# Attention by halves of the heads with the scores four rounds ahead, and a feed-forward second pass in written order with one PSUM bank per chunk

## The chip, the cores and the metric

The kernel runs on one core of a Trainium2 chip. The metric is the device time of one execution in microseconds. The core's engines are PE (TensorE, matrix products and transposes), DVE (VectorE), ACT (ScalarE), POOL (GpSimd) and SP (SyncE, which issues DMAs). Each works off its own queue in order; semaphores tie the queues together. [...]

## The reference, cut to what matters

Two layers are applied to `x` of shape (16, 256, 256), 16 batches of 256 rows. All products below are in fp32 unless another type is named.

```python
# layer 0: masked attention of 16 heads of 16 columns, keys = values = ctx
scores = einsum('bqhd,bkhd->bhqk', layernorm(x) by heads, ctx by heads)
scores = where(mask == 0, -1e20, scores)
out = softmax(scores / 16) @ ctx by heads
x = x + out @ W_out.T + b_out

# layer 0: quantised feed-forward, 256 -> 1024 -> 256
# quant_act: s = max(t) / 255 over the WHOLE tensor; round(t / s) clipped to 0..255
h = relu(quant_act(layernorm(x)) @ int8(w1).T + b1)
x = x + quant_act(h) @ int8(w2).T + b2

# layer 1: attention by lags: the correlation of q and k over all circular lags,
# the six best lags over the batch mean, a softmax over them, v delayed by each lag
x = x + delayed_sum(layernorm(x) @ Wq, ctx @ Wk, ctx @ Wv) @ Wo + bo
# layer 1: mixture of experts, 8 experts of which each row takes 2, and a shared one
x = x + shared(x) + routed(x)
```

The largest value of `h` over all rows is needed before any of `h` can be rounded. So the feed-forward part computes its first product twice: once to find the maximum, once to use it.

## The kernel before, in words

The rows lie in `x` as 32 tiles of 128; a batch is two tiles (`QT` = 2) and a feed-forward block is four tiles of 128 rows (`NB` = 8 blocks). The span has four stages: attention to about 426 us, feed-forward to about 580 us, the lag attention to about 641 us, and the mixture of experts to the end, which the diff does not touch.

**Attention.** A batch `b` is prepared by `prep`: `cxp` (L433) is the context spread out for the heads, `qp` (L442) the normalised rows, `kT` and `qT` are their transposes on PE, copied out of PSUM by ACT (`turn`, L371 and L376; from batch 3 on `turn_close`, L387), and `mbT` (L481, L482) is the transposed mask. The softmax needs the largest score of each row and head. `largest(b, r)` computes a quarter of the scores: eight matmuls `sp` (L500) into two tiles of two banks of the pool `ps_w` (three such tiles), and eight maxima on DVE (L511) into `mx`. Before, `qt, gp = divmod(r, 2)`, so quarters 0 and 1 are the two halves of the heads for the first tile of rows. `shift(b)` takes the finished maxima: DVE writes them negated into `mxc` (L531), PE transposes it (`mxtp`, L540), and DVE adds the result to `qT` (L549, one instruction of 128 x 1024). After that `weights(b, g)` can run: the shifted scores `st` (L568), the mask added by matmuls (L578), and two exps on ACT (L588, `pT`). `values(b, g)` multiplies them with the context (`o`, L601; copied to `oT`, L610). `finish(b)` transposes (`otp`, L619), divides by the sums (`ri` L626, `on` L627, DVE), transposes again (`ontp`, L637), projects (`pp`, L651) and adds to `x` (L655, DVE). `summary` takes layer-norm statistics and a row maximum (`rmax`, L663). 

The 64 rounds `n = 4b + r` are written by hand, and PE keeps the written order: one list of jobs for each of the four slots of a batch. `largest` runs five rounds ahead, at the front of a slot. In slot 3 of batch `b` stand, in order: `largest(b+2, 0)`, `shift(b+1)`, the values of the round before, the weights of this round with a piece of `finish` between its exps. The order on DVE, ACT, POOL and SP is a scheduler's, which starts from the order of emission and heeds priorities (`high_priority`) and `issue_after`; `behind()` puts side work behind the last maximum emitted. Side work is spread over the slots: `rest`, the preparation of other weights on PE (`turn_weight`, eight and four pieces; `product` and the bias row `bvo`, L299 to L306, a chain on DVE), `ints` (rounding of the int8 weights on DVE, L189 to L213), and `ahead` (statistics of later batches). All small transposes share one bank (tag "m").

**Startup.** `prep(0)`, then scores of rounds 0 to 3 of batch 0 with `prep(1)` between them, then `shift(0)`, then the loop.

**Feed-forward.** The first pass computes `ph` (two matmuls `first`, L916, for each of eight chunks and each block) in tiles of two banks, and DVE takes maxima (`hmax`, L1013, one for two chunks). Between them `keys1` turns the context of a batch into keys for layer 1 (`ctp` L931, `cT` L934, `pk` L944, `gT` L952); ten in the pass, two after it. `values1` (`pv`, L961 and L963) does the same for values. A chain on DVE and POOL (L1030 to L1051) then turns the maximum into scales. In the second pass PE has no written order: `hidden` computes two chunks into one two-bank tile (`ps_h`, two tiles), ACT applies the relu (L1060), DVE rounds (`hq`, L1068). `second` multiplies by `w2` (`py`, L1076), ACT writes `yT` (L1083), PE transposes it (`ytp`, L1092), DVE adds it to `x` (L1097) and takes statistics.

**Lag attention.** Normalised rows `xn` are transposed (`x2tp`, L1179) and multiplied; three `values1` stand before it, seven cover the choice of the lags and a DMA of the matrices `cm` (L1303), which the products `po` (L1307) wait for.

Of the kernel before, what the change touches and what calls it, by code (L numbers as in the profile page):

```python
# [18 lines left out]
P = 128  # L19
# [9 lines left out]
def tile_kernel(ctx: ExitStack, tc: tile.TileContext, io: dict, out: bass.AP):  # L29
# [121 lines left out]
    with tc.tile_pool(name="pa", bufs=2) as pa, tc.tile_pool(  # L151
# [69 lines left out]
        def turn_weight(wT, who):  # L221
            while who not in integers:
                yield
            q = integers[who]
            oc_n, ic_n = q.shape[1], q.shape[2] // P
            for oc in range(oc_n):
                for i0 in range(0, ic_n, 4):
                    n = min(4, ic_n - i0)
                    tp = mtile([P, n, P], f"wt_{who}_{oc}_{i0}", BF16)
                    for i in range(n):  # L230
                        nc.tensor.transpose(
                            tp[:, i, :], q[:, oc, (i0 + i) * P : (i0 + i + 1) * P], ident16
                        )
                    nc.scalar.copy(wT[:, i0 : i0 + n, oc * P : (oc + 1) * P], tp)
                    if oc + 1 == oc_n and i0 + n == ic_n:
                        integers[who + "_turned"] = True
                    yield
# [39 lines left out]
        def pair_weights():  # L277
# [22 lines left out]
            nc.vector.memset(bvo3, 0.0)  # L300
            for i in range(3):
                part = pa.tile([P, D], BF16, tag="bvo_part", bufs=1, name=f"bvo_part{i}")
                nc.vector.tensor_copy(part, left)
                nc.vector.tensor_copy(bvo3[32 * i : 32 * i + 1, :], part[32 * i : 32 * i + 1, :])
                if i < 2:
                    nc.vector.tensor_tensor(left, left, part, ALU.subtract)  # L306
            yield
# [18 lines left out]
        def stats_ahead():  # L326

            yield
            yield
            for b0, b1 in [(3, 4)] + [(b, b + 2) for b in range(4, B, 2)]:  # L330
                for b in range(b0, b1):
                    for t in range(b * QT, (b + 1) * QT):
                        ln_stats(mv0, t)
                    yield
                ln_rstd(rstd0, mv0, b0 * QT, (b1 - b0) * QT, "0", scale)
                yield
                for _ in range(0 if b0 == 3 else 5):
                    yield
# [27 lines left out]
        def turn(dst, src, g0, name):  # L366

            tp = mtile([P, 2, QT, P], f"{name}_tp")
# [50 lines left out]
        def prep(b):  # L419
# [32 lines left out]
            with behind():  # L452
                nc.vector.tensor_scalar(mb, mi, 0.0, MASKED, ALU.is_equal, ALU.mult)
# [13 lines left out]
            else:  # L467
                turn(kT, cxp, 0, f"kT{b}")
                yield
                turn(kT, cxp, 2, f"kT{b}")  # L470
                yield
            if b == 0:
                turn(qT, qp, 0, f"qT{b}")
                yield
                turn(qT, qp, 2, f"qT{b}")
                yield
# [9 lines left out]
            if 0 < b < 3:  # L486
# [5 lines left out]
        def largest(b, r):  # L492

            pr = seqs[b]
            qt, gp = divmod(r, 2)
# [11 lines left out]
            for j in range(4):  # L507
                for g in range(2):
# [12 lines left out]
                    if j == 1:  # L521
                        order["half"] = done

        def shift(b):
# [3 lines left out]
            if b < 2:  # L528
                nc.gpsimd.memset(mxc, 0.0)
            with tc.high_priority():  # L530
                nc.vector.tensor_scalar(  # L531
                    mxc[:, :, :, HD : HD + G],
                    pr["mx"].rearrange("p t (g j) -> p t j g", g=G),
# [4 lines left out]
            tp = mtile([P, QT, P], f"mxtp{b}")  # L538
# [4 lines left out]
            with ExitStack() as where:  # L543
                where.enter_context(tc.high_priority())
                if b > 0:
                    where.enter_context(tc.issue_after(order["half"]))
                for gs in (slice(0, 1), slice(1, G)) if b == 0 else (slice(0, G),):
                    to = pr["qT"][:, gs, :]
                    done = nc.vector.scalar_tensor_tensor(  # L549
                        to,  # L550
                        to,
                        keep,
                        tp.rearrange("p t q -> p (t q)").unsqueeze(1).to_broadcast(to.shape),
                        ALU.mult,
                        ALU.add,
                    ).ins
            if b == 0:
                order["last"] = done
# [33 lines left out]
        def values(b, g, pTs):  # L592

            pr = seqs[b]
            if g == 0:
                pr["oT"] = pa.tile([P, G, S], F32, tag="oT", name=f"oT{b}")
            if g % 2 == 0:
                pr["o"] = ps_o.tile([P, 2, S], F32, tag="o", name=f"o{b}_{g}")
            for k in range(QT):
# [9 lines left out]
            if g % 2 == 1:  # L609
# [67 lines left out]
        first_prep = prep(0)  # L677
        piece(first_prep)
        load_x(1, 2)
        for _ in range(3):  # L680
            piece(first_prep)
        largest(0, 0)
        piece(first_prep)
        with behind():
            stats0(1, 2)
        first_prep = prep(1)
        piece(first_prep)
        largest(0, 1)
        piece(first_prep)
        piece(first_prep)  # L690
# [4 lines left out]
        largest(0, 3)  # L695
# [106 lines left out]
        for _ in shift(0):  # L802
            pass
        with behind():
            stats0(2, 3)
        load_x(5, 9)
        pend = None
        for b in range(B + 1):
            nxt = prep(b + 2) if b + 2 < B else rest
# [4 lines left out]
            jobs = [  # L814
                ((nxt,), (rest,), (fin,)),
                ((nxt,), (nxt,), (fin,)),
                ((fin,), (rest,), (fin,)),
                ((shf,), (), (fin,)),
            ]
            if b == 0:  # L820
                jobs = [
                    ((), (), (first_prep,)),
                    ((nxt,), (nxt,), (nxt,)),
                    ((nxt,), (nxt,), (rest,)),
                    ((rest,), (shf,), (rest,)),
                ]
            for r in range(4):

                n = 4 * b + r
                front, later = {0: ([], [4]), 1: ([5], [6])}.get(  # L830
                    n, ([n + 5] if n + 5 < 4 * B else [], [])
                )
                for m in front:
                    largest(*divmod(m, 4))
                for job in jobs[r][0]:
                    piece(job)
                if pend is not None:
                    values(*pend)
                for job in jobs[r][1]:
                    piece(job)  # L840
                pend = (b, r, []) if b < B else None
                wts = weights(*pend) if b < B else None
                piece(wts)
                for job in jobs[r][2]:
                    piece(job)
                piece(wts)
                if n == 0:
                    piece(first_prep)
                for m in later:
                    largest(*divmod(m, 4))  # L850
                with behind():
# [3 lines left out]
                    if b > 0 and r != 2:  # L855
                        piece(ints)
                if r == 0 and b % 4 == 0 and b + 9 < B:
# [3 lines left out]
        for _ in rest:  # L861
            pass
# [19 lines left out]
    with tc.tile_pool(name="pb", bufs=2) as pb, tc.tile_pool(  # L882
        name="ps_h", bufs=2, space=PSUM
    ) as ps_h, tc.tile_pool(name="ps_b", bufs=2, space=PSUM) as ps_b, tc.tile_pool(
        name="ps_y", bufs=2, space=PSUM
    ) as ps_y:
# [27 lines left out]
        def first(blk, ph, fc):  # L914
            for c in range(DC):
                nc.tensor.matmul(  # L916
# [5 lines left out]
                )  # L922
# [59 lines left out]
        def integers_of(blk):  # L982
            qi = pb.tile([P, TB, D], BF16, tag="qi", name=f"qi{blk}")
            for i in range(TB):
                t = blk * TB + i
                u = pb.tile([P, D], F32, tag="u", bufs=4, name=f"u{t}")
# [16 lines left out]
        with tc.manual_schedule(engines={mybir.EngineType.PE}):  # L1003
            for _ in integers_of(0):
                pass
            key = None
            for blk in range(NB):
                ahead = integers_of(blk + 1) if blk + 1 < NB else iter(())
                for f0 in range(0, FC, 2):
                    ph = ps_h.tile([P, 2, 512], F32, tag="h", name=f"ph1_{blk}_{f0}")  # L1010
                    for f in range(2):
                        first(blk, ph[:, f, :], f0 + f)
                    nc.vector.tensor_reduce(  # L1013
                        hmax[:, f0 : f0 + 2, blk], ph, axis=AX.X, op=ALU.max
                    )
                    if f0 < 4:
                        next(ahead, None)
                    if key is not None:
                        next(key)
                        key = None  # L1020
                    elif f0 == 2 or (f0 == 6 and blk % 4 == 0):
                        key = keys1(next(keyed))
                        next(key)
        for b in keyed:
            for _ in keys1(b):
                pass
# [26 lines left out]
        def hidden(blk, hq, f0):  # L1053

            ph = ps_h.tile([P, 2, 512], F32, tag="h", name=f"ph2_{blk}_{f0}")
            for f in range(2):
                fc = f0 + f
                first(blk, ph[:, f, :], fc)
                h32 = pb.tile([P, 512], F32, tag="h32", bufs=4, name=f"h32_{blk}_{fc}")
                nc.scalar.activation(  # L1060
                    h32,
                    ph[:, f, :],
                    AF.Relu,
# [742 lines left out]
```

## Time and profile before

| | us |
|---|---|
| median of three runs | 1407.86 |
| lowest, highest | 1406.86, 1409.86 |
| the profiled execution, its own time | 1407.56 |
| its span in the trace | 1405.9 |
| PE busy | 1358.8 |
| DVE busy | 633.8 |
| ACT busy | 553.3 |

The span runs from the first instruction to the last; 1.66 us of the profiled execution lie around it. A window's row in the trace gives its length, then the busy time of each engine in it with the number of instructions in brackets, then the clock that TensorE was granted (1.00 is full speed), the share of the DMA engines, and GB/s. A timeline row gives start and length in us, the engine, the line, the operation, what it writes and reads with shapes, how many instructions it joins, and in square brackets how long the engine stood idle before it and what ended that. A matmul at half clock counts as busy for all of its longer time.

### The profile page before, as it was taken

Reading aid. Unit: us, or ns where it says so; the run is one execution under the profiler, and the core shown is the slowest. Engines: PE = TensorE matmul, PEld = TensorE weight load, DVE = VectorE, ACT = ScalarE, POOL = GpSimd, SP = SyncE. Lnnn points to the kernel's source line nnn. Section 1 sums busy time; section 2 is a strip of 40 time slices with the busy share of each in tenths; the row PEclk is TensorE's granted clock in tenths of the full one; section 3 lists DMA queues with packets and bytes.
Section 4 is the critical chain, followed back from the end, with each engine's and each line's share of the span. In section 5 each row is a group of like instructions: output and inputs, shape, how many; then the busy total and the mean of one; then the engine's idle time right before and its main releaser. Section 6 shows DMA issues by size and latency. Waiting matters only on the chain. (4 is left out here: it accounts for less than half of the span.)

```text
span 1405.9 us, 24030 instructions
## 1 busy us (share of the span) xinstructions
PE 1358.8 (97%) x8881; PEld 1035.8 (74%) x8955; DVE 633.8 (45%) x2520; ACT 553.3 (39%) x1050; POOL 239.0 (17%) x312
## 2 busy tenths in 40 slices
PE   6999999999989999999999999999999999999998
PEld 3565655666647644678788888888888888888887
DVE  7688879887737868857830101011011110101025
ACT  1454545554447568423622222323322323222221
POOL 6232133122000000000026530111111111111110
PEclk9899999999999999999999999999999999999999
DMA  9231323221001100333002245767666767665246
GB/s 276 78 96 54 105 85 91 70 73 27 17 18 37 45 0 1 112 98 96 3 31 83 72 156 195 249 231 244 244 248 233 246 236 257 234 232 190 96 155 220
DMA packets 127831, 184.06 MB, mean 131 GB/s; under 512 B 11600, under 2 KB 104952, under 8 KB 127712
## 3 DMA queue, kind: packets, MB, share of 16 engines
q1 hardware_dynamic: 117600, 152.55, 33.6%
q0 software_dynamic: 10112, 29.94, 6.1%
q8 instruction: 72, 1.18, 0.3%
q14 instruction: 47, 0.39, 0.1%
HBM read 141.16 MB, written 34.48 MB: 125 GB/s over the span
## 5 line engine op out<-in xcount | busy, mean ns | idle before, releaser
L1415 ACT ACTIVATE hTr<-pfr,bsel 128x256 f32<-128x256 f32 (+1 forms) x344 | 147.6, 430 | 345.9 <-PE pfr L1407 337.1
L1653 PE MATMUL ppr<-wp,hTr 128*128 128x256 f32 x1088 | 248.5, 379 | 0.0
L1407 PE MATMUL pfr<-xjT,wf 128*128 128x256 f32 (+1 forms) x1376 | 246.6, 338 | 0.7 <-DVE xjT L1643 0.7
L1407 PEld LDWEIGHTS pfr<-xjT,wf 128*128 128x128 f32 x1376 | 215.8, 191 | 30.3 <-issue 9.9
L1661 DVE TENSOR_TENSOR yj<-ppr,bj 128x512 f32<-128x512 f32 (+1 forms) x43 | 24.9, 580 | 440.3 <-PE ppr L1653 440.3
L1653 PEld LDWEIGHTS ppr<-wp,hTr 128*128 128x128 f32 x1088 | 202.1, 190 | 25.0
L511 DVE CUSTOM_DVE_ANT_0 junk<-sp,mb 128x256 bf16<-128x256 f32 x512 | 182.8, 420 | 37.6 <-PE sp L500 37.3
L588 ACT ACTIVATE pT<-st 128x1024 f32<-128x1024 f32 x128 | 124.4, 1021 | 125.9 <-PE st L578 125.9
L1679 POOL DMA_INDIRECT ys_d<-yj,to x68 | 65.4, 962 | 454.3 <-DVE to L1670 241.4
L1415 ACT ACTIVATE hTs<-pfs,bcol 128x256 f32<-128x256 f32 x128 | 59.9, 474 | 140.7 <-PE pfs L1407 137.5
L1407 PE MATMUL pfs<-xnT,wf-1_7251 128*128 128x256 f32 x512 | 114.5, 380 | 0.1
L1449 PE MATMUL pps<-wp-1_7253,hTs 128*128 128x256 f32 x496 | 109.6, 379 | 0.3 <-DVE x L1463 0.3
L1407 PEld LDWEIGHTS pfs<-xnT,wf-1_7251 128*128 128x128 f32 x512 | 96.4, 190 | 14.1 <-issue 1.4
L1449 PEld LDWEIGHTS pps<-wp-1_7253,hTs 128*128 128x128 f32 x496 | 94.2, 190 | 13.5 <-DVE x L1463 0.7
L500 PE MATMUL sp<-kT,qT 16*128 16x256 f32 x1024 | 93.4, 422 | 2.3 <-DVE mx L511 2.0
L568 PE MATMUL st<-qT,kT 32*128 32x256 f32 x1024 | 78.6, 404 | 0.7 <-DVE qT L549 0.7
L500 PEld LDWEIGHTS sp<-kT,qT 16*128 16x128 f32 x1024 | 59.2, 193 | 25.3 <-DVE mx L511 8.4
L1580 POOL DMA_INDIRECT xs_d<-xn,slot_i x64 | 61.8, 966 | 89.4 <-ACT hTs L1415 46.3
L601 PE MATMUL o<-pT,cxp 128*32 128x256 f32 x1024 | 73.6, 397 | 1.3 <-ACT pT L588 1.3
L916 PE MATMUL ph<-qT,w1T 128*128 128x512 bf16 x245 | 68.4, 378 | 4.0 <-DVE hmax L1013 1.4
L1463 DVE TENSOR_TENSOR x<-pps,x 128x512 f32<-128x512 f32 x15 | 10.4, 690 | 124.8 <-PE pps L1449 124.8
L568 PEld LDWEIGHTS st<-qT,kT 32*128 32x128 f32 x1024 | 50.7, 186 | 18.2 <-issue 12.4
(308 smaller groups left out, 1626.3 us busy)
## 6 DMA issues: line engine op xcount, KB each, us to landing
wf<-in_L_ffn_Wfc_dram SPq DMA_DIRECT2D x43, 1024.0 KB
wp<-in_L_ffn_Wproj_dram SPq DMA_DIRECT2D x43, 1024.0 KB, 5.7
xs_d<-zero POOLq DMA_DIRECT2D x36, 258.0 KB
yg<-ys_d SPq DMA_DIRECT2D x16, 512.0 KB, 6.4
xj<-xs_d SPq DMA_DIRECT2D x25, 258.0 KB
bj<-in_L_ffn_bproj_dram SPq DMA_DIRECT2D x43, 128.0 KB, 9.7
x<-in_x_dram SPq DMA_DIRECT2D x16, 256.0 KB, 10.7
cx<-in_ctx_dram SPq DMA_DIRECT2D x16, 256.0 KB, 2.7
```

The lines of the kernel that those rows point to most:

```text
L500: nc.tensor.matmul(sps[j // 2][:, j % 2, g, :], pr["qT"][rows, 2 * gp + g, qt * P : (qt + 1) * P], pr["kT"][rows, 2 * gp + g, :], start=Tr ...
L511: order["last"] = done = nc.vector.tensor_tensor_reduce(out=junk, in0=sps[j // 2][:, j % 2, g, :], in1=pr["mb"][:, qt, :], scale=1.0, scal ...
L568: nc.tensor.matmul(tps[j // 2][:, j % 2, k, :], pr["kT"][rows, g, k * P : (k + 1) * P], pr["qT"][rows, g, :], start=(k == 0), stop=False, ...
L588: nc.scalar.activation(pT, tps[i], AF.Exp)
L601: nc.tensor.matmul(pr["o"][HP * j : HP * (j + 1), g % 2, :], pr["cxp"][:, k, 4 * g + j, :], pTs[j // 2][:, j % 2, k, :], start=(k == 0), s ...
L916: nc.tensor.matmul(ph, w1T[:, c, fc * P : (fc + 1) * P], qT[:, c, blk * 512 : (blk + 1) * 512], start=(c == 0), stop=(c == DC - 1),)
L1407: nc.tensor.matmul(ph, wf[:, c, fc * P : (fc + 1) * P], rhs[:, c, :], start=(c == 0), stop=(c == DC - 1),)
L1415: nc.scalar.activation(hT[:, fc, :n], ph, AF.Gelu_apprx_tanh, bias=bias[:, fc : fc + 1]).ins
L1449: last = nc.tensor.matmul(po[:, i, :], hT[:, fc, i * P : (i + 1) * P], wp[:, fc, :], start=(fc == 0), stop=(fc == FC - 1),).ins
L1580: ins = nc.gpsimd.indirect_dma_start(out=xs_d, out_offset=bass.IndirectOffsetOnAxis(ap=slot_i[:, k, t : t + 1], axis=0), in_=xn3[t // QT][ ...
L1653: nc.tensor.matmul(po[:, i, :], hT[:, fc, i * P : (i + 1) * P], wp[:, fc, :], start=(fc == 0), stop=(fc == FC - 1),)
L1679: nc.gpsimd.indirect_dma_start(out=ys_d, out_offset=bass.IndirectOffsetOnAxis(ap=to[:, i : i + 1], axis=0), in_=yj[:, i, :], in_offset=None,)
```

## The change

In attention:

- `gp, qt = divmod(r, 2)`: rounds 0 and 1 of a batch are now the same half of the heads for both tiles of rows, so that half has all of its maxima after two rounds.
- At the start, `shift(0)` is done in two halves, the second after `largest(1, 0)`. The turns of `prep(0)` go to tiles of `ps_w`, and `prep(1)` is interleaved with `prep(0)`. `mxc` is cleared earlier, on POOL, and `load_x(5, 9)`, the load of the rows of batches 5 to 8, is issued in round 1 instead of ahead of the loop.
- In the loop, `largest` runs four rounds ahead, at the end of a slot. In slot 3 the order is now: half of the values, a piece of `finish`, the weights, the other half of the values, `shift(b+1)`, `largest(b+2, 0)`. On DVE the `qT` update stands directly behind `mxc`, ahead of all maxima of `largest(b+2, 0)`; before, it stood after the fourth of them.
- One piece of `rest` for each batch, in slot 2, where there were two. `turn_weight` does eight transposes and one copy in a piece. The `bvo` chain is cut in four pieces, its clearing on POOL. Statistics of batches 2 and 3 are taken together in the first loop.

In feed-forward and after:

- `keys1` runs twice in every second block of the first pass (before: in every fourth), and twelve lie in the pass. One `values1` follows the pass.
- The second pass has a pool `ps_k` of four tiles of one bank, and PE's order is written: for each chunk its two matmuls, two products `py` of the block before, and one transpose `ytp` of the block before that. Each chunk's first matmul is put behind the relu of the chunk before in the order of instructions, without a wait. `values1` stands also after chunk 3 of block 0 and after the last products.
- `rstd2` is computed in three bursts (after blocks 3 and 6, and in the next stage). The normalised rows of the first block, `xn_first`, are written during block 5. The buffer `u` has three copies, before four.
- The lag attention begins with one `values1` (before: three), and six are left at its end (before: seven).

The diff, cut to its core:

```diff
-            for oc in range(oc_n):
-                for i0 in range(0, ic_n, 4):
...
+            step = 8 // ic_n
+            for oc in range(0, oc_n, step):
+                tp = mtile([P, ic_n, step, P], f"wt_{who}_{oc}", BF16)
...
-            nc.vector.memset(bvo3, 0.0)
+            nc.gpsimd.memset(bvo3, 0.0)
+            yield
             for i in range(3):
...
+                with behind():
...
+                yield
...
+                tps = [
+                    ps_w.tile([P, 2, 2, S], F32, tag="w", name=f"{n}T0_tp") if b == 0 else None
+                    for n in "kq"
+                ]
+                turn(kT, cxp, 0, f"kT{b}", tps[0])
...
-            qt, gp = divmod(r, 2)
+            gp, qt = divmod(r, 2)
...
-        def shift(b):
+        def shift(b, gs=slice(0, G)):
...
-            with ExitStack() as where:
-                where.enter_context(tc.high_priority())
-                if b > 0:
-                    where.enter_context(tc.issue_after(order["half"]))
...
+            with tc.high_priority(), tc.issue_after(order["some"]):
+                to = pr["qT"][:, gs, :]
...
-        def values(b, g, pTs):
+        def values(b, g, pTs, ks=range(QT)):
...
-        for _ in shift(0):
+        for _ in shift(0, slice(0, G // 2)):
             pass
+        largest(0, 3)
+        piece(p1)
+        largest(1, 0)
         with behind():
-            stats0(2, 3)
-        load_x(5, 9)
+            stats0(2, 4)
...
-            jobs = [
-                ((nxt,), (rest,), (fin,)),
-                ((nxt,), (nxt,), (fin,)),
-                ((fin,), (rest,), (fin,)),
-                ((shf,), (), (fin,)),
-            ]
...
+                slots = [
+                    ["sums", nxt, "weights", fin, "more", 5],
+                    [nxt, "sums", nxt, "weights", fin, "more", 5],
+                    [fin, "sums", rest, "weights", fin, "more", 5],
+                    ["sums, some", fin, "weights", "sums, rest", "more", shf, 5],
+                ]
...
-                u = pb.tile([P, D], F32, tag="u", bufs=4, name=f"u{t}")
+                u = pb.tile([P, D], F32, tag="u", bufs=3, name=f"u{t}")
...
-                    elif f0 == 2 or (f0 == 6 and blk % 4 == 0):
+                elif f0 == 2 or (f0 == 6 and blk % 2 == 0):
...
+        ps_k = first_pass.enter_context(tc.tile_pool(name="ps_k", bufs=4, space=PSUM))
...
-        def hidden(blk, hq, f0):
-
-            ph = ps_h.tile([P, 2, 512], F32, tag="h", name=f"ph2_{blk}_{f0}")
...
+        def hidden(blk, hq, fc):
+
+            ph = ps_k.tile([P, 512], F32, tag="k", name=f"ph2_{blk}_{fc}")
+            first(blk, ph, fc, relus[-1] if relus else None)
...
+            for fc in range(FC):
+                hidden(blk, hq, fc)
+                next(mul, None)
+                next(turn, None)
+                if blk == 0 and fc == 3:
+                    values1(next(valued), ps_b, "b")
...
-        for _ in range(3):
-            values1(next(valued), ps_c, "c")
+        values1(next(valued), ps_c, "c")
```

A number `5` in a slot of the new list is `largest` of round `n + 5`, now at the slot's end, where four whole slots lie between it and that round. `mul` is the generator of `second`, which now yields after every two products, and `turn` that of `turned`, which yields after every transpose.

## The prediction

> **What bounds the kernel now.** I read the engines' totals first, then the slices, then windows of 20 us, and the timeline only where the windows leave PE short.
>
> ```profile
> PE 1358.8 (97%) x8881; PEld 1035.8 (74%) x8955; DVE 633.8 (45%) x2520; ACT 553.3 (39%) x1050; POOL 239.0 (17%) x312
> PE   6999999999989999999999999999999999999998
> DVE  7688879887737868857830101011011110101025
> ```
>
> PE (the matmul engine) is the bound; only 47 us of the span are not PE. DVE's digits show where it is nearly as full: the first 17 slices, some 600 us, which hold attention and the feed-forward part. From about 640 us on, the 20 us windows hold 20 us of PE. The change touches only what is before that, so its worth is PE's holes there, and PE's half-speed stretches, which count as busy.
>
> ```profile
> 0.00:20.00 20.00, 11.20 (x60) 7.19 (x61) 13.47 (x64) 5.74 (x10) 15.24 (x40) 1.00 0.85 232
> 20.00:40.00 20.00, 13.83 (x85) 7.90 (x85) 15.17 (x81) 3.63 (x6) 12.60 (x20) 0.97 1.05 336
> 40.00:60.00 20.00, 18.87 (x154) 10.71 (x156) 11.86 (x67) 7.58 (x11) 0.00 (x0) 0.77 0.11 35
> 180.00:200.00 20.00, 18.17 (x178) 11.08 (x182) 17.04 (x69) 8.02 (x10) 11.04 (x13) 0.91 0.42 129
> 500.00:520.00 20.00, 18.48 (x80) 8.54 (x82) 10.15 (x31) 14.99 (x24) 0.00 (x0) 1.00 0.00 0
> ```
>
> After the window and its length stand PE, weight loads, DVE, ACT, POOL, the granted clock. The first 60 us lose 16.1 us of PE; 180 to 200 loses 1.8 at a clock of 0.91; 500 to 520 loses 1.5. PE's timeline says how:
>
> ```profile
> 30.17 0.66 PE L540 MATMUL mxtp<-ident,mxc 128*128 128x128 f32 x2 [2.52 <-DVE mxc L531]
> 31.49 2.09 PE L568 MATMUL st<-qT,kT 32*128 32x256 f32 x16 [0.66 <-DVE qT L549]
> 46.02 1.15 PE L568 MATMUL st<-qT,kT 32*128 32x256 f32 x16
> 195.94 1.09 PE L387 MATMUL qT_tp<-ident,qp 128*128 128x128 f32 x4 [1.11 <-DVE on L627]
> 196.96 1.94 PE L601 MATMUL o<-pT,cxp 128*32 128x256 f32 x16
> 508.57 0.59 PE L916 MATMUL ph<-qT,w1T 128*128 128x512 bf16 x2
> 509.02 0.81 PE L1076 MATMUL py<-hq,w2T 128*128 128x512 bf16 x3
> 510.03 0.59 PE L916 MATMUL ph<-qT,w1T 128*128 128x512 bf16 x2 [0.20 <-ACT h L1060]
> ```
>
> The same 16 matmuls take 2.09 us at 31 us and 1.15 at 46; round (0,1) starts only at 46.02. At 196 a late DVE costs a stall and then half speed. In the second feed-forward pass PE waits for ACT each time.
>
> **Startup: about -8.0.** Round (0,1)'s weights start at 46.02. The new order on PE up to there, by half-speed rows (turn of four 1.11, scores 2.09, mask transposes 0.6, values 1.94): batch 0's k turns end at 8.1 as now, batch 1's first k turn takes the place of the 0.94 wait for qp, the q turns end near 12.7 and scores (0,0) near 14.8. The rest of batch 1's turns (3.3), the mask (0.6) and scores (0,1), (0,2) fill PE to about 22. Now PE stands 2.52 until all 32 maxima are in; the half shift needs only 16, and scores (0,3) and (1,0) and the last turn lie between the halves. So weights (0,0) start at about 30, with scores (1,0) already done, and (0,1) after the mask (0.6), scores (1,1) (2.09) and values (0,0) (1.94): 30 + 3.9 (weights at half speed) + 4.6 = 38.5. That is 7.5 sooner. Batch 2's two k turns, which stood before 46.02, now come later: 2 x 0.58 at full speed, 1.2 given back. The second half-speed stretch of before (values 1.94 for 1.07 at 52.98, two turns of 0.86 and 1.12 for 0.58 each, about 1.7 together) I count as gone. -7.5 + 1.2 - 1.7 = -8.0. Bounds: -4 (the two turns in one ps_w tile still wait for each other's copy, 0.68 twice, and half speed stays) and -10. The memsets of mxc (0.34 each) move ahead on POOL into its 1.74 us wait for cx; load_x(5,9), later on SP's queue, is for batches whose stats come tens of us later; stats0(2,4) adds 3.3 us to DVE, which sits idle 4.47 us and more here. All three: nothing, at most 1 us each if that cover goes.
>
> **The bvo row: -2.75.** One DVE burst (memset, casts, subtracts, 2.66 us of chain at 191.4 to 195.0) makes `on` late. PE loses 1.11, the turn 0.51, the values 0.87, and the output transposes about 0.26 to half speed. Cut into pieces of 0.7 to 0.9 it fits in DVE's gaps. At worst 0.
>
> **Steady rounds: +2.5.** Work is unchanged: a batch is 4 x (scores 1.08 + values 1.00 + weights 1.96) + 5.4 of transposes and projections = 21.6 of PE. The start of mxtp from batch to batch (61.2 to 391.9, 14 periods) averages 23.6; the rest is background transposes and the 1.51 us scores behind an exp, which stay. New is a tighter place. Before, about 7 us of PE lay between scores (b+1,3) and mxtp, and 7 again up to weights (b+1,0). Now mxtp has half the values 0.53 + projection 0.95 + weights 1.96 + half the values 0.53 = 4.0 ahead of it; DVE must do 8 maxima (2.76), x add 0.35, rmax 0.60, mxc 0.15 = 3.9, beginning some 0.3 before the scores end. Behind mxtp 2.7 of PE (scores, values, a turn) cover the 1.28 us qT update. So an idle DVE is in time by 0.4, and any backlog beyond that becomes PE's stall. Backlog comes in the batches with rstd chains and weight quantisation: with them DVE holds 5.4 to 6.8 us between two score groups where PE has 5.6 plus a background piece. I take 0.4 us over six such batches, +2.5. PE behind a waiting mxtp holds the next scores, and ACT's exps wait for those. Bounds: -3 (the 0.59, 0.40 and 1.45 waits on x L655 go) and +8 (0.6 in each of 14). The transposes of w1 and w2 in pieces of eight and one `rest` per batch move PE's fill, not its sum: 0. The tail (rounds of 4.8 to 5.0 at 393 to 426) has the same waits on exp and `on`: 0, from -1.5 to +1.
>
> **Feed-forward: -7.0.** Last matmul of the first pass to first x2tp is 495.75 to 579.93, 84.2 us. Each block of the second pass takes 9.0 (ytp at 513.75, 522.72, 531.71). Its pure PE is 32 x 0.2155 + 8 x 0.11 = 7.8; ACT has 8 relus of 0.725 and two yT of 0.78, 7.4. With a bank per chunk and products in between, PE should set the pace: 8 x 7.8 = 62.4, four values1 of 1.96 = 7.8, and 2 us of filling: 72.2. The maxima's chain (497.0 to 499.1) is covered by one values1 and four chunks, 1.96 + 1.72. But two keys1 that lay behind the pass now lie in it, 2 x 2.2 = 4.4, and DVE, 90% full there, gets slack in exchange. 84.2 - 72.2 - 4.4 = 7.6; I take 7.0, since 7.4 of ACT in 7.8 leaves little. Bounds -8.5 and -4 (block 8.2). xn_first and the bursts of rstd lie on a DVE with 6 us per block: nothing, or 1 us each if a burst stands before an hq.
>
> **Smaller.** One values1 fewer covers the wait for cm ahead of the delays: now 641.28 without a wait, while the last cm lands not before 640.5; 1.96 gone leaves 1.2 to 1.8 as stall: +1.5. Three u buffers for four: 0 to +2, taken +0.5, as qi is two tiles ahead.
>
> **Sum.** -8.0 - 2.75 + 2.5 + 0 - 7.0 + 1.5 + 0.5 = -13.25. The profiled run took 1407.56 (span 1405.9 and 1.66 around it), within 0.3 of the median 1407.86. 1407.6 - 13.3 = 1394.3.
>
> [...] The row: after one stall of 1.11 us the window 196 to 200 has a clock of 0.59. [...] By the row such a stall costs 2.75, and 14 of them 38. The trace decides, and the sum goes by the row; so the tight place is what this change risks.
>
> **Rivals.**
> - Half as good. DVE is late by 0.5 at every shift, +7 in place of +2.5, and ACT keeps blocks at 8.2, +3.4: 1394.3 + 7.9 = 1402. For it: ACT's 7.4 of 7.8, DVE's 17 to 18 of 20 us in the windows from 60 to 200. Against: DVE is only 12 of 20 by 380. Chance 0.2.
> - Better. Full PE from 22 us opens the clock before 35, startup -10; steady rounds lose their x L655 waits, -1; FFN -8.5: sum -10 - 2.75 - 1 - 8.5 + 1.5 + 0.5 = -20.3, 1387. For: at 42 to 46 a busy stretch was followed by full speed. Chance 0.12.
> - It doesn't do what it says: relu is ACT's chain, the block stays 9.0 (8 x 1.2 = 9.6 back), the shared tile turns still wait (+4): 1408. For: the second copy uses the same tile. Against: ACT idles 0.69 after each pair of relus. Chance 0.06.
> - Slower: the tight shift alone. If DVE is over 0.4 late at mxtp it stalls PE, and if that half-closes the clock each event costs like the bvo row, 2.75. It decides from 15.8 us together (13.25 + 2.5), 1.1 per batch; at 1.4 in 14 batches, 19.6: 1411. For: 0.4 of slack by the sum above. Against: 1.1 late in every batch needs more backlog than half of them have. Chance 0.12.
> - The forecast: 0.50.
>
> **Numbers.** Faster than 1405 by over 0.2% (2.8 us, about what a measurement of this kernel can tell from no change): 0.50 + 0.20 + 0.12 = 0.82; within: 0.06; slower: 0.12. The range leaves out the slower cases and the far end of the better one: 1384 to 1405.
>
> **What the changed profile would show.** Right: round (0,1)'s weights at 37 to 40 us, no window with a clock under 0.9 between 180 and 200, mxtp waiting under 0.5 in most batches, ytp 7.8 to 8.0 apart, a wait of 1 to 2 for cm ahead of `po`. Wrong: mxtp waiting over 1 us for mxc in most batches, clocks of 0.6 to 0.9 in several windows from 80 to 380, or ytp still 9.0 apart.

## The result, and the profile after

The changed kernel takes 1396.2 us (median of six, 1394.73 to 1400.61); the kernel before took 1407.36 beside it (six, 1405.23 to 1410.23). The ratio is 0.9935, interval 0.9917 to 0.9952: faster by 0.65%, inside the range of the forecast (1394.3; 1384 to 1405) and 2 us above its number. The profiled execution of the changed kernel was the slowest of the six, 1400.61, with a span of 1398.9. That it was the slowest is part of what follows.

The totals and the slices of the page of after:

```profile
PE 1365.3 (98%) x8957; PEld 1034.8 (74%) x8957; DVE 626.8 (45%) x2454; ACT 552.4 (39%) x1042; POOL 238.7 (17%) x313
PE   7999999999989999999999999999999999999998
DVE  8688878877746868847730101011011110101025
```

The sums of PE do not compare closely: the trace of before has 76 matmul records fewer at the same work, and half clock counts as busy. The slices and the windows do (columns as in the prediction):

```profile
0.00:20.00 20.00, 12.08 (x63) 8.36 (x64) 15.44 (x81) 5.78 (x10) 14.09 (x32) 1.00 0.82 231
20.00:40.00 20.00, 19.02 (x115) 9.98 (x113) 17.98 (x83) 3.71 (x5) 12.42 (x27) 1.00 1.06 316
40.00:60.00 20.00, 18.04 (x186) 10.43 (x182) 9.64 (x48) 9.67 (x14) 5.74 (x7) 0.98 0.17 56
180.00:200.00 20.00, 20.00 (x202) 12.21 (x206) 13.21 (x62) 9.86 (x13) 0.72 (x1) 1.00 0.45 128
220.00:240.00 20.00, 17.69 (x174) 9.94 (x173) 16.13 (x58) 8.16 (x10) 8.30 (x11) 0.91 0.28 84
260.00:280.00 20.00, 17.61 (x178) 9.78 (x175) 17.38 (x73) 7.89 (x11) 7.75 (x9) 0.94 0.13 31
520.00:540.00 20.00, 20.00 (x105) 10.94 (x103) 15.55 (x47) 18.52 (x27) 0.00 (x0) 1.00 0.00 1
```

The hole at 20 to 40 is filled, the one at 180 to 200 is gone, the second pass at 520 to 540 is full. But 220 to 240 and 260 to 280 each lost more than 2 us, and these windows were full enough before (18.96 and 19.52).

I divide each span at three rows that all kernels have: the first `ph`, the first `x2tp`, the first `po`. So "attention" here also holds the work between the last round and the first `ph`. In us:

| profiled execution | attention | feed-forward | lag attention | experts | span |
|---|---|---|---|---|---|
| before | 440.2 | 139.7 | 61.4 | 764.6 | 1405.9 |
| after | 443.7 | 130.8 | 61.2 | 763.2 | 1398.9 |
| e1, feed-forward alone | 440.9 | 130.8 | 60.9 | 762.5 | 1395.1 |
| e2, attention alone | 434.1 | 139.7 | 61.3 | 763.9 | 1399.1 |
| e4, no mxc instruction | 433.4 | 130.8 | 61.1 | 762.6 | 1388.0 |
| e10, best | 429.7 | 130.8 | 61.2 | 762.8 | 1384.5 |

Feed-forward gained 8.9 us, the same in all four that have the new one. In this execution of the changed kernel attention lost 3.5 us, where the forecast had it gain 8.25; in the trace of e2, which has the same attention, it gained 6.1. One trace does not say what the new attention is worth. The 1.5 in the experts, which the diff does not touch, is within what that stage varies by: e4 and e6 (below) are the same program there, and their traces have 762.6 and 765.3.

### The profile page after: what moved, and what is told of

Same layout as the page of the kernel before. It is cut to its first block, busy times and chain, and to the rows that moved or that the text cites. A ratio compares the mean times of both kernels' runs of the same rounds, so it can differ in the third digit from the quotient of the medians.

```text
span 1398.9 us, 24064 instructions
## 1 busy us (share of the span) xinstructions
PE 1365.3 (98%) x8957; PEld 1034.8 (74%) x8957; DVE 626.8 (45%) x2454; ACT 552.4 (39%) x1042; POOL 238.7 (17%) x313
## 5 line engine op out<-in xcount | busy, mean ns | idle before, releaser
L619 PE MATMUL o<-pT,cxp 128*32 128x256 f32 x1024 | 76.7, 401 | 0.9 <-ACT pT L606 0.9
L526 PEld LDWEIGHTS sp<-kT,qT 16*128 16x128 f32 x1024 | 59.0, 196 | 19.6 <-issue 10.5
L596 PE MATMUL st<-mbT,ident 128*128 128x512 bf16 x256 | 67.2, 385 | 0.0
```

The lines of the kernel that those rows point to most:

```text
L526: nc.tensor.matmul(sps[j // 2][:, j % 2, g, :], pr["qT"][rows, 2 * gp + g, qt * P : (qt + 1) * P], pr["kT"][rows, 2 * gp + g, :], start=Tr ...
L596: nc.tensor.matmul(tps[i][:, j].rearrange("p k q -> p (k q)"), ident16, pr["mbT"].rearrange("p k q -> p (k q)"), start=False, stop=True, s ...
L619: nc.tensor.matmul(pr["o"][HP * j : HP * (j + 1), g % 2, :], pr["cxp"][:, k, 4 * g + j, :], pTs[j // 2][:, j % 2, k, :], start=(k == 0), s ...
```

## The experiments

**What holds the shift.** The timeline of after has the waits, on PE first:

```profile
225.46 0.44 PE L564 MATMUL mxtp<-ident,mxc 128*128 128x128 f32 x2 [2.31 <-DVE mxc L555]
227.35 1.94 PE L619 MATMUL o<-pT,cxp 128*32 128x256 f32 x16
276.29 0.44 PE L564 MATMUL mxtp<-ident,mxc 128*128 128x128 f32 x2 [2.39 <-DVE mxc L555]
326.42 0.44 PE L564 MATMUL mxtp<-ident,mxc 128*128 128x128 f32 x2 [0.82 <-DVE mxc L555]
```

DVE's rows of `mxc`, and POOL's rows at the same times:

```profile
222.63 2.77 DVE L555 TENSOR_SCALAR mxc<-mx 128x32 f32<-128x32 f32 x1
250.26 0.18 DVE L555 TENSOR_SCALAR mxc<-mx 128x32 f32<-128x32 f32 x1
273.38 2.85 DVE L555 TENSOR_SCALAR mxc<-mx 128x32 f32<-128x32 f32 x1
325.08 1.28 DVE L555 TENSOR_SCALAR mxc<-mx 128x32 f32<-128x32 f32 x1
```
```profile
222.58 2.77 POOL L665 TENSOR_TENSOR x<-x,row_L_xattn_b_out 128x256 f32<-128x256 f32 x4
273.41 2.77 POOL L665 TENSOR_TENSOR x<-x,row_L_xattn_b_out 128x256 f32<-128x256 f32 x4
323.54 2.78 POOL L665 TENSOR_TENSOR x<-x,row_L_xattn_b_out 128x256 f32<-128x256 f32 x4
```

`mxc` is 32 numbers per partition and takes 0.18 us. Three times it lasted until POOL's run of four bias additions ended: 222.63 + 2.77 = 225.40 against 225.35, 276.23 against 276.18, 326.36 against 326.32. It waits for no semaphore of POOL there. So DVE was not late with its work. The instruction had started and was held. The two half shifts of batch 0 show the same: the first `mxc` lasted 1.70 us, until POOL's copy of `cxp` ended (22.24 against 22.20), the second 0.69, until the additions at the start ended (30.17 against 30.13).

Two kernels test this, against a backlog of DVE. e3 leaves the additions out:

```diff
-            for t in range(QT):
-                nc.gpsimd.tensor_tensor(xb[:, t, :], xb[:, t, :], bout_row, ALU.add)
```

> The changed kernel without POOL's additions of the output bias to x in attention (the bias is left out). Theory A (mxc, a tensor_scalar on DVE, stood 2.77 and 2.85 us while POOL ran four additions, 222.58 to 225.35 and from 273.41; nothing else made it late): no mxc over 0.3 us from the third batch on, no mxtp wait over 0.5, all executions at 1393 to 1396. Rival B (DVE's backlog in the batches with rstd and weight quantisation makes mxc late): mxtp still waits 1 to 2.5 us in one to three batches, and executions spread to 1400.

e4 keeps them and takes the held instruction away. Each maximum goes straight to its place in `mxc`, and the `qT` update subtracts:

```diff
-                        accum_out=pr["mx"][:, qt, h : h + 1],
+                        accum_out=mxcs[b % 2][:, qt, j, HD + 2 * gp + g : HD + 2 * gp + g + 1],
...
-                nc.vector.tensor_scalar(
-                    mxc[:, :, :, HD + gs.start : HD + gs.stop],
...
-                    ALU.add,
+                    ALU.subtract,
```

> The changed kernel with each maximum written directly into its place in mxc, and the qT update subtracting: no mxc instruction, POOL's additions stay. Theory A: DVE has no instruction at this place that POOL can hold, so no mxtp wait over 0.5 us and all executions at 1392 to 1395. Rival B (backlog): mxtp waits fall by the 0.2 of mxc and the 0.6 of rmax alone, waits of 1.5 us stay in one to three batches, 1395 to 1399.

e3 took 1389.75 us (1387.57 to 1391.13; ratio 0.9883, 0.9863 to 0.9904), e4 1390.39 (1389.68 to 1392.75; 0.9896, 0.9879 to 0.9913). In e3 `mxc` is short in the same three batches:

```profile
220.37 0.18 DVE L555 TENSOR_SCALAR mxc<-mx 128x32 f32<-128x32 f32 x1
267.21 0.18 DVE L555 TENSOR_SCALAR mxc<-mx 128x32 f32<-128x32 f32 x1
315.01 0.18 DVE L555 TENSOR_SCALAR mxc<-mx 128x32 f32<-128x32 f32 x1
```

In e4 POOL's additions run across the same place, from 221.33, and the shift does not wait:

```profile
221.33 2.79 POOL L656 TENSOR_TENSOR x<-x,row_L_xattn_b_out 128x256 f32<-128x256 f32 x4
```
```profile
221.82 0.44 PE L555 MATMUL mxtp<-ident,mxc 128*128 128x128 f32 x2
268.67 0.44 PE L555 MATMUL mxtp<-ident,mxc 128*128 128x128 f32 x2
316.46 0.44 PE L555 MATMUL mxtp<-ident,mxc 128*128 128x128 f32 x2
```

Theory A held and the backlog fell. With DVE's other work as it was, no shift from the third batch on waits. (The first `mxc` of e3 still lasts 1.44 us, until POOL's copy of `cxp`, which e3 keeps: 22.27 against 22.24.) The size was better than I wrote: I expected 1393 to 1396 for e3 and 1392 to 1395 for e4.

**The parts alone.** e1 has the old attention and the new rest of the program, e2 the new attention and the old rest; both are the two files joined behind attention, with no other edit.

> Attention as before; feed-forward and lag attention as changed. Theory (the two parts add up; stage by stage the changed trace lost 2.6 us in the first pass, gained 11.6 from there to x2tp and 0.1 after): about 9 us faster than before, 1397 to 1400. Rival (the feed-forward's new order needs the new attention's earlier end, or part of the gain lies at the end of the program, where the changed trace was 1.5 shorter): 6 us or less.

> Attention as changed; feed-forward and lag attention as before. Theory (the new attention is worth about 4 us, and executions in which mxc on DVE is held up by POOL's bias add lose 2 to 3 us for each such event): 1402 to 1406, with a spread of some 6 us between executions, the slowest no better than before. Rival (attention gains the 8.25 us of the forecast and the changed trace was an outlier): 1399, spread as before.

e1 took 1395.34 us (1394.24 to 1397.94; 0.9925, 0.991 to 0.9941), e2 1402.96 (1400.6 to 1412.64; 0.999, 0.9972 to 1.0008), both beside 1406.65. Feed-forward alone is as fast as the whole change. What attention adds is not told by these runs: e2's median is 3.7 us under before's, inside the 1402 to 1406 of the theory, but the interval of its ratio reaches past 1. Its twelve executions spread over 12 us, twice what I expected, and its slowest is slower than any of before; no trace shows a slow one, so what slowed them stays open. The execution that was profiled is one of the three fastest. In it the three hold-ups come to PE as waits of 0.25, 0.33 and 0.82 us, in after as 2.31, 2.39 and 0.82. POOL's additions and `mxc` meet in the same three batches in both:

```profile
267.81 0.79 DVE L555 TENSOR_SCALAR mxc<-mx 128x32 f32<-128x32 f32 x1
267.84 2.79 POOL L665 TENSOR_TENSOR x<-x,row_L_xattn_b_out 128x256 f32<-128x256 f32 x4
```

But here `mxc` was through after about one addition (0.79 us, and 0.71 at 220.64), where in after it stood through all four. So what differs from one execution to the next is how long the hold lasts; what decides that, no run shows. It goes with 7.1 us between the second shift and the sixteenth: 331.3 in e2, 338.4 in after. e1's 11.3 us is more than the 9 expected; its trace shows 10.8, of which 2.1 lie in the experts.

**What makes the second pass faster.** After's timeline of it, one chunk after another without a wait:

```profile
518.03 0.59 PE L943 MATMUL ph<-qT,w1T 128*128 128x512 bf16 x2
518.46 0.59 PE L1111 MATMUL py<-hq,w2T 128*128 128x512 bf16 x2
518.89 0.29 PE L1136 MATMUL ytp<-ident,yT 128*128 128x128 f32 x1
519.02 0.59 PE L943 MATMUL ph<-qT,w1T 128*128 128x512 bf16 x2
```

A chunk takes 0.97 and a block 7.8. Two things changed at once, the order and the banks (a bank is counted here as the tile of 128 x 512 fp32, 2 KB a partition, that holds one chunk's `ph`). e7 leaves PE's order to the scheduler (on top of e4, as all that follow). From here on a median beside e4's is a rough measure: e4 stood beside a before of 1406.65, e5 to e8 beside one of 1404.82, e9 to e11 beside one of 1406.17. Where a stage of the traces decides, I give it.

```diff
         first_pass.close()
+        ordered.close()
```

> e4 with the second feed-forward pass's order on PE left to the scheduler as before, the bank per chunk kept. Theory (the gain of 1.2 us per block came from the order: products of the block before between the chunks; the scheduler puts one product of the same block behind each chunk): blocks of 8.3 to 9.0, 4 to 9 us more than e4. Rival (the four single banks alone free PE from ACT): blocks of 7.8, the time of e4 within 1 us.

It took 1392.45 us (1391.4 to 1392.52; 0.9917, 0.9903 to 0.9931), 2 more than e4, and its blocks are 7.8. The 2 lie in attention (435.8 for 433.4 in the traces), which the edit does not touch; feed-forward is 130.8 in both. The written order as such was not the cause: emitted chunk by chunk, the scheduler's order is nearly the same. e9 keeps the order and goes back to tiles of two banks:

```diff
-            ph = ps_k.tile([P, 512], F32, tag="k", name=f"ph2_{blk}_{fc}")
+            if fc % 2 == 0:
+                pairs[0] = ps_k.tile([P, 2, 512], F32, tag="k", name=f"ph2_{blk}_{fc}")
+            ph = pairs[0][:, fc % 2, :]
```

> e4 with the second feed-forward pass in the same written order, but in tiles of two banks for two chunks (two such tiles), as before, in place of a bank per chunk. e7 showed that PE's written order is not needed. Theory (the single banks are: a chunk can start once its own bank's relu is done, with two banks it waits for the second relu of a pair): blocks of 8.4 to 9.0, 4 to 9 us more than e4. Rival (products of the block before, taken two at a time between single chunks, give ACT the time it needs, whatever the tiles are): blocks of 7.8, within 1 us of e4.

It took 1419.53 us (1417.06 to 1420.02; 1.009, 1.0073 to 1.0108), 29 more than e4, slower than the kernel before. Its timeline on PE:

```profile
531.28 0.59 PE L934 MATMUL ph<-qT,w1T 128*128 128x512 bf16 x2 [0.69 <-ACT h L1092]
532.25 0.59 PE L934 MATMUL ph<-qT,w1T 128*128 128x512 bf16 x2
533.71 0.59 PE L934 MATMUL ph<-qT,w1T 128*128 128x512 bf16 x2 [0.33 <-ACT h L1092]
534.68 0.59 PE L934 MATMUL ph<-qT,w1T 128*128 128x512 bf16 x2
536.51 0.59 PE L934 MATMUL ph<-qT,w1T 128*128 128x512 bf16 x2 [0.70 <-ACT h L1092]
```

Four chunks take 5.23 us, a block 10.5, well over the 8.4 to 9.0 of my theory; feed-forward took 158.3 for 130.8. At each new pair PE waits for a relu, and behind that wait stand, in the written order, the products that could have run. With tiles of two banks this order loses, with a bank per chunk it does not. Two things stay open. The relu that ends the wait is that of the chunk just before (530.45 + 0.78 = 531.23), though there are two such tiles; why two tiles give PE no lead, no run shows. And a bank per chunk with chunks emitted in pairs, as before, was not run.

**The rest of attention.** e5 undoes the split of the values in slot 3:

```diff
-                    ["sums, some", fin, "weights", "sums, rest", "more", shf, 5],
+                    ["sums", fin, "weights", "more", shf, 5],
```

> e4 with the values of slot 3 in one piece ahead of the weights. In the changed trace the values of a batch took 4.16 us, before 4.00 (start to start), since each of the two pieces ends in a gap, and the projections 2.01 for 1.91. Theory (the pieces cost PE and hide nothing at the shift, which has the same work ahead of it either way): 2 to 3 us less than e4, about 1388. Rival (the second half of the values fills PE while exp runs and the bank of the small transposes comes free; without it mxtp waits): mxtp waits 0.3 to 0.6 in each batch, 3 to 6 us more than e4, 1394.

1393.68 us (1393.23 to 1394.7; 0.993, 0.9916 to 0.9943): 3.3 more than e4, and 3.4 more in the attention of its trace. My theory was wrong, and the rival right in size but not in place. `mxtp` does not wait. The scores behind it do: 1.79 us for 1.15, as they need a tile that the exp still reads. The batch takes 23.33 for 23.12. The half of the values between weights and shift covers that exp.

e6 moves batch 2's last turn out of the way of the second shift:

```diff
-                    ["sums", "weights", "p2", "more", 6, "p2"],
+                    ["sums", rest, "weights", "p2", "more", 6, "p2"],
...
-                    ["sums", rest, "weights", "p2", "more", shf, 8],
+                    ["sums", "p2", "weights", "more", shf, 8],
```

> e4 with batch 2's last q turn moved from between the exps of round (0,3) to ahead of its weights, and the background piece there moved two slots up. Theory (the 1.7 us that the second shift waited for ACT's copy of this turn, behind two exps, and the half clock after it go): no wait of mxtp over 0.5 at 52 to 58, clock 1.00 from 45 to 80, 1.5 to 2.5 us less than e4, about 1388.5. Rival (the shift waits for DVE's maxima there in any case): the wait is named mxc, under 0.5 us less than e4.

1390.99 us (1388.07 to 1393.74; 0.9901, 0.9884 to 0.9918). The 1.70 us wait and the half clock behind it went, as expected (its granted clock is 1.00 from 40 to 80 us, e4's 0.94 and 0.98), but the median did not move. The trace, of e6's slowest execution, says where it went. Its weights of round (0,1) start 3.7 us later than e4's (43.74 for 40.01): 1.6 of it stood already at the first scores, the rest came with half speed until about 45 us, in e4 until 37. From these weights to the first `ph` e6 takes 390.9 us and e4 393.4, the 2.5 that the theory gave at most. So the start hides what e6 won; five executions do not separate the two medians.

e11 puts the `bvo` chain back in one piece, clearing included (the diff's `bvo` part undone):

```diff
-            nc.gpsimd.memset(bvo3, 0.0)
-            yield
+            nc.vector.memset(bvo3, 0.0)
             for i in range(3):
-                with behind():
...
-                yield
+            yield
```

> e4 with the bvo chain in one piece on DVE again, its clearing too. Theory (the forecast's term: one burst of 2.7 us makes a wait of 1.1 and a stretch at half clock): one PE wait of 1 to 2.5 us behind DVE in that batch, 1.5 to 3.5 us more than e4. Rival (in the new order the burst falls where DVE has room): no such wait, within 0.7 us of e4.

1390.1 us (1388.75 to 1392.6; 0.9889, 0.9871 to 0.9908): as e4. In the new order the chain runs at 332.42, not 191.42, and no shift or turn waits behind it. That fewer side jobs fall there is argued, not shown: DVE is busy 16.17 of the 20 us from 320, and was 17.04 of those from 180 in before.

e8 takes away the `values1` that opens the lag attention, so that seven cover the wait for `cm`:

```diff
         queue = []
-        values1(next(valued), ps_c, "c")
```

> e4 without the values1 at the start of the lag attention, so that seven stand again ahead of the delays. Theory (x2tp of the first block has its rows ready, and the 1.6 to 1.75 us wait for cm is covered): 1 to 1.8 us less than e4, about 1389. Rival (that values1 covers the wait for the last blocks' statistics, 0.8 us on DVE's x, and for ACT's copies): x2tp begins less than 1 us sooner and the time is that of e4.

1391.28 us (1390.39 to 1392.31; 0.9913, 0.9898 to 0.9929), no gain. `po` no longer waits for `cm`, but 0.68 us for a copy of ACT, where e4 waited 1.70. Its timeline shows two waits at the place of that `values1`:

```profile
562.84 1.09 PE L1237 MATMUL x2tp<-ident,xn_first 128*128 128x128 f32 x8 [0.81 <-DVE x L1133]
565.34 3.72 PE L1250 MATMUL pm<-q,gT 128*128 128x256 f32 x16 [1.41 <-DVE q L1240]
```

The first is not new: e4 has it too, 0.81 us at 562.28, ahead of the `values1`. The second is: there e4 waits 0.16. So that `values1` covers the making of `q`, and what is won at `po` is lost here. The rival had the time right and the wait wrong.

**A better version.** e10 is e4 and e6, and batch 0 keeps `mx` and the `mxc` instruction (with factor 1), so that its first half shift does not wait for the second half's maxima:

```diff
-                        accum_out=pr["mx"][:, qt, h : h + 1],
+                        accum_out=pr["mx"][:, qt, h : h + 1]
+                        if b == 0
+                        else mxcs[b % 2][:, qt, j, HD + 2 * gp + g : HD + 2 * gp + g + 1],
```

> e4 and e6 together, and batch 0 alone keeps its separate maxima and the mxc instruction, so that its first half shift need not wait for the maxima of scores (0,2) (in e4 it waited 3.03 us, in the changed kernel not). Theory: weights (0,0) 1.5 to 3 us sooner than in e4, no mxtp wait over 0.5 anywhere, 1386 to 1389. [...]

1386.97 us (1386.19 to 1393.56; 0.9871, 0.985 to 0.9892): the lowest median, 1.3% under the kernel before, though its interval overlaps that of e4. Weights (0,0) start 1.4 us sooner than in e4 (30.64 for 32.00), a little less than I expected, and the first half shift still waits 0.69. The second shift starts at 53.60 without a wait, where after had

```profile
57.56 0.44 PE L564 MATMUL mxtp<-ident,mxc 128*128 128x128 f32 x2 [1.70 <-ACT qT L387]
```

## Why the prediction was right, and where it was not

The total is right, and in part by luck. For feed-forward and what follows up to `po` I had -5.0, and the traces show -9.1; for attention I had -8.25, and it gained 6.1 in one execution and lost 3.5 in another. The forecast's place of the gain, more than half of it in attention, was wrong.

- **Feed-forward, -7.0: right, and better.** From the end of the first pass to `x2tp` I had 84.2 down to 72.2; the rows give 84.4 (495.57 to 579.93) and 72.0 (502.55 to 574.54), from the start of the instruction behind the pass. Of the 4.4 for two `keys1` inside the pass only 3.4 came (55.4 to 58.8); that DVE's slack took back the rest is a guess. So 8.9, and the caution that brought 7.6 down to 7.0 was not needed: ACT's 7.4 of 7.8 was enough.
- **Cover for cm, +1.5: wrong sign.** The wait came at its size:

```profile
635.75 12.32 PE L1375 MATMUL po<-cT,cm 128*128 128x256 f32 x56 [1.75 <-DMA cm<-cd]
```

  But the `values1` that no longer stands there was already paid for in the 72.2. The stage has 1.96 less work and 1.75 more wait, -0.1 in all (61.35 to 61.21). I priced the loss of a cover and forgot that the cover was moved work. The +0.5 for `u` did not show.
- **Startup, -8.0: mis-sized.** Weights (0,0) start at 30.90, as forecast (30), but take 5.0 us for the 3.9 that I had, and weights (0,1) start at 40.38 (forecast 38.5, before 46.02). At the second shift after is 3.6 us sooner (57.56 for 61.19), with one round of weights more (1.96) and one of scores less (1.08) behind it: 4.5 in all. I counted the second half-speed stretch as gone. It came back, for a reason that I had not looked for: the second shift shares the bank of the small transposes with batch 2's turn, whose copy waits behind two exps on ACT (the 1.70 above). At 59.0 the values then take 1.69 for 1.07. In e10, without that wait, the shift is 7.6 us sooner with the same work behind it, 8.5 in all. Part of that is the clock: full speed came at about 36 us in e10 and 42 in after. In e2, with after's attention and the same 1.70, the second shift came at 55.58, 6.5 in all. So 4.5 to 6.5 of the 8.0 came in the version as changed, and the rest is there to be had.
- **bvo, -2.75: the loss went, by another edit.** 180 to 200 is full. e11 shows that cutting the chain is not why: the slower pace of `rest` moved it, and at its new place the whole chain costs nothing that can be told. Nor was the clearing part of the burst that I read: in before it ran at 4.88.
- **Steady rounds, +2.5: mis-sized, and for the wrong reason.** From the second shift to the sixteenth before took 330.7 us, with the loss at bvo in it, after 338.4, e2 331.3, e4 329.6. In e3 and e4 no shift waits in that stretch, so the tight place of itself makes no wait: with PE 4.0 ahead and DVE 3.9, DVE was in time in every batch, those with rstd and weight quantisation too. The term that I put at 0.4 us of backlog in six batches was no backlog. What costs is one instruction, `mxc`, that POOL can hold. In the profiled execution that was 5.5 us of waits, and some 2.7 of half speed behind the first two (values 1.94 for 1.07 twice, turns 1.01 and 1.12 for 0.58). The medians of after and e4 are 5.8 apart (5.1 when each is set against the before beside it), about what it costs in a usual execution; in that of e2's trace it was 1.4 of waits. e4 also saves the 0.2 of `mxc` itself.
- **The slower rival** had the right place, the right sequel (half speed after the wait) and the wrong cause. It needed 1.1 us in every batch; after has 2.3 twice and 0.8 once in fourteen. (In the first rival, eight blocks at 8.2 for 7.8 are 3.2 us, not 3.4.)
- **Half speed behind a wait.** After has the like of before's row three times: waits of 2.31 at 225.46 and 2.39 at 276.29, each followed by values of 1.94 us for 1.07, and one of 1.70 at 57.56, followed by values of 1.69, with a granted clock of 0.50 from 60 to 62. But it does not follow on every such wait: in before one of 1.45 at 139.00 was followed by a turn of 0.66 and values of 1.07, at a granted clock of 1.00 from 139 to 147. So to price each wait like the bvo row was an estimate from one case; what decides, no run shows.

By what means POOL holds `mxc`, no run shows. The rows show that `mxc` ends within 0.05 us of POOL's end three times, and that e3 and e4 each remove the wait from one side. In after DVE stood twice through four of POOL's instructions in a row (2.77 us, 0.69 each), in e2 twice through one. At 222.63 its row starts 0.05 us behind that of POOL's additions, at 273.38 it starts 0.03 us ahead of them, and it was held both times.

## What to carry to other kernels

When a step is moved to where an engine has just enough time, look at every instruction on that short path for what else can hold it, not only at the engine's load: a VectorE instruction of 0.18 us, held for up to 2.85, here cost nearly all of what attention had to gain, because GpSimd was at work at the same time (in e3, without GpSimd's additions, it took 0.18 in the same three batches). If such an instruction can be folded into its producer, as the maxima were here, the collision goes without anything being moved. And when a cover is taken away, write down where the covering work went before pricing the wait that it uncovers.

## What the runs showed of the hardware that I had not expected

- A VectorE tensor_scalar of 0.18 us lasted 2.77 and 2.85 us while GpSimd ran four two-input additions, and 0.71 and 0.79 at the same places in another execution (e2); the maxima, which read PSUM, went on at their 0.345 us beside the same additions (e4), and so did the `qT` update at its 1.28.
- Full clock came at about 42 us in after, 37 in e4 and 45 in e6, at nearly the same work. By an estimate from these 8 us at half speed that is worth up to 4 us between executions, as much as most of the edits here. The times are read from the length of the rows: the profile's clock column shows 1.00 from 0 to 40 us of after, where the same 16 scores took 2.09 us and later 1.15.
- Two PSUM banks in one tile, with a fixed order on PE, chunk by chunk, made a block 10.5 us, where single banks gave 7.8 and two banks with the scheduler's order 9.0 (the kernel before).
